# A graph attention layer: its lead-in ordered by a list scheduler with the work dealt anew, and the next to last output part finished beside the last products

## The chip, the core and the metric

One of the cores of a Trainium2 chip runs the kernel: TensorE (PE), VectorE (DVE), ScalarE (ACT) and GpSimd (POOL) compute, SyncE (SP) issues DMAs, and ACT and POOL issue some as well. Each engine runs its own instructions in the order in which they are written, and waits on semaphores where an instruction needs another engine's work. The metric is the device time of one execution in microseconds (us), as the median of several runs.

## The reference, cut to what matters

12,500 nodes with 128 features, 412,500 edges sorted by target with 64 features each, four heads of 32. Layer norm and ReLU of the nodes, a linear layer, an attention logit for each edge, a softmax over the edges of a target (which also counts the edges that are not there), a weighted sum of source rows, and the input added back:

```python
h = jnp.maximum(_layernorm(x, axis=-1), 0.0)
...
h = (node_features @ W_node.T).reshape(num_nodes, H, HD)
e = (edge_features @ W_edge.T).reshape(num_edges, H, HD)
...
att = jnp.sum(jnp.concatenate([h[src], h[tgt], e], axis=-1) * a, axis=-1)
att = jnp.where(att > 0, att, 0.2 * att)
m = jnp.maximum(jax.ops.segment_max(att, tgt, num_segments=num_nodes), 0.0)
ex = jnp.exp(att - m[tgt])
denom = segment_sum(ex, tgt) + (num_edges - deg)[:, None] * jnp.exp(-m)
return x + segment_sum((ex / denom[tgt])[:, :, None] * h[src], tgt)
```

## The kernel before, in words

**The lead-in** turns x into a table in DRAM with one row of 144 numbers a node: for each head 32 products, two ones and two logit parts. x goes through in 98 blocks of 128 rows. Blocks form groups (`sizes`, L304), up to `XB` = 9 of them, and each group has units of `XS` = 3 blocks. A group is loaded by a DMA on SP's queue (`load_rows`, L307, five buffers `xg`). A unit's steps, each by a function of its own:

- `measure` (L328, DVE): `bn_stats` of each block, and behind the group's last unit four small instructions that combine them (L337 to L341)
- `root` (L345, ACT) and `deviate` (L351, DVE): for a group, one over the standard deviation, and the shift
- `normalize` (L357): a block each on ACT (L366) or POOL (L363); units take turns with two on ACT and one on POOL, or one and two
- `turn` (L369, PE): each block transposed into PSUM tile `pt`, which is one bank with up to three blocks (three such tiles)
- `keep_turned` (L375, DVE): ReLU of the whole unit into `hT`
- `project` (L379, PE): the product with `wall`, into PSUM tile `ph` (two matmuls a block in the trace, as for every float32 matmul)
- `keep_rows` (L384): copy to `rows` on ACT (L389), and the ones by a memset on DVE (L390)
- `write` (L393): when a group is whole, its table rows by a DMA on ACT's queue, and the target logits copied to `tn` on DVE (L396)

`wall` is made from the weights by a transpose, a small matmul with `a_diag` and three copies on DVE (L425 to L435). The order of all that is a loop written by hand (from `ahead, lag = 7, 3`, L420): at unit k it projects unit k, normalises and transposes unit k + 3, measures up to unit k + 7, and applies the ReLU last. Behind the loop come `keep_near` (the target logits transposed and stored), `load_extents` and `chunk_ranges` (bounds of the edge chunks, DVE for the most part).

**The batches.** 67 batches of edges follow. For each, POOL issues 49 indirect DMAs (`gather`, L631; the last batch has fewer) that fetch table rows of the source nodes into one of four buffers `hs`. DVE and ACT make the weights, DVE multiplies the rows by them (L814), PE adds them up by target (L819), and `merge` adds what was collected to `acc` (L926). Before the first gather lies the whole table, since any row may be asked for.

**The tail.** The last batch is done in two parts (`first_part`, `second_part`). Ahead of `second_part`, `close` of the batch before merges its sums, runs `finish` (L987) for the output part that is then complete, whose stores go out on SP and ACT, and moves the open sums to the front of `acc` (`shift_sums`: a copy on DVE, L866, and a memset on POOL, L867). `second_part` then computes the weights of the last half batch (from L729), multiplies (L796), sums on PE (L803), copies the sums on ACT (L789, L790), and the last `close` merges and finishes the last part.

Of the kernel before, what the change touches and what calls it, by code (L numbers as in the profile page):

```python
# [18 lines left out]
P = 128  # L19
# [29 lines left out]
XS = 3  # L49
R = 2 * SB * H  # L50
# [75 lines left out]
def kernel(  # L126
# [110 lines left out]
    with (  # L237
# [65 lines left out]

        sizes = [XS, XS, 2 * XS] + [XB] * ((NB - 4 * XS) // XB)  # L304
        sizes += [XS, NB - sum(sizes) - XS]

        def load_rows(b0, n):  # L307

            s = Rows()
            s.b0, s.n = b0, n  # L310
            full = min(n, (N - b0 * P) // P)
            s.x = p3.tile([P, XB, D], F32, name="xg", bufs=5)
            nc.sync.dma_start(s.x[:, :full, :],
                              x[b0 * P:(b0 + full) * P, :].rearrange("(b p) d -> p b d", p=P))
            if full < n:
                nc.vector.memset(s.x[:, full, :], 0.0)
                rest = N - (b0 + full) * P
                nc.sync.dma_start(s.x[:rest, full, :], x[(b0 + full) * P:N, :])
            s.stats = p2.tile([P, XB, 2, 3], F32, name="stats", bufs=5)
            s.units = []  # L320
            for i0 in range(0, n, XS):
                u = Rows()
                u.s, u.i0, u.m = s, i0, min(XS, n - i0)
                s.units.append(u)
            return s


        def measure(u):  # L328
            s = u.s
            for i in range(u.i0, u.i0 + u.m):  # L330
                nc.vector.bn_stats(s.stats[:, i, :, :].rearrange("p a b -> p (a b)"), s.x[:, i, :])  # L331
            if u is not s.units[-1]:
                return

            n = s.n
            tot = p2.tile([P, XB, 2], F32, name="tot", bufs=5)
            nc.vector.tensor_tensor(tot[:, :n, :], s.stats[:, :n, 0, 1:], s.stats[:, :n, 1, 1:], op=OP.add)  # L337
# [5 lines left out]
            measured.append(s)  # L343

        def root(s):  # L345
            n = s.n
            s.rstd = p2.tile([P, XB], F32, name="rstd", bufs=5)
            nc.scalar.activation(s.rstd[:, :n], s.var, AF.Sqrt, bias=eps, scale=1.0 / D)
            rooted.append(s)
# [7 lines left out]
        def normalize(u):  # L357
            s = u.s
            u.hn = p2.tile([P, XS, D], F32, name="hn", bufs=4)
            for i in range(u.m):  # L360
                k = slice(u.i0 + i, u.i0 + i + 1)
                if i == XS - 1 or (i and (s.b0 + u.i0) // XS % 2):
                    nc.gpsimd.tensor_scalar(u.hn[:, i, :], s.x[:, k, :].rearrange("p b d -> p (b d)"),  # L363
                                            s.rstd[:, k], s.shift[:, k], op0=OP.mult, op1=OP.add)
                else:
                    nc.scalar.activation(u.hn[:, i, :], s.x[:, k, :].rearrange("p b d -> p (b d)"), AF.Identity,  # L366
                                         scale=s.rstd[:, k], bias=s.shift[:, k])

        def turn(u):  # L369
            pt = pps.tile([P, XS, P], F32, name="pt", bufs=3)  # L370
            for i in range(u.m):
                nc.tensor.transpose(pt[:, i, :], u.hn[:, i, :], ident)  # L372
            u.pt = pt

        def keep_turned(u):  # L375
            u.hT = p2.tile([P, XS, P], F32, name="hT", bufs=5)
            nc.vector.tensor_scalar(u.hT[:, :u.m, :], u.pt[:, :u.m, :], 0.0, None, op0=OP.max)  # L377
# [6 lines left out]
        def keep_rows(u):  # L384
# [5 lines left out]
            nc.vector.memset(rows.rearrange("p b (h k) -> p b h k", h=H)[:, :, :, HD:HD + 2], 1.0)  # L390
            return s if u is s.units[-1] else None

        def write(s):  # L393
            nc.scalar.dma_start(table[s.b0 * P:(s.b0 + s.n) * P, :].rearrange("(b p) c -> p b c", p=P),
                                s.rows[:, :s.n, :])
            nc.vector.tensor_copy(tn[:, s.b0:s.b0 + s.n, :],  # L396
# [12 lines left out]
        groups, units, measured, rooted = [], [], [], []  # L409

        def load_next():
            if len(groups) < len(sizes):
                s = load_rows(starts[len(groups)], sizes[len(groups)])
                groups.append(s)
                units.extend(s.units)

        for _ in range(5):
            load_next()
        early = [index(b) for b in range(2)]
        ahead, lag = 7, 3  # L420
        measure(units[0])
        root(measured.pop())
        deviate(rooted.pop())
        measure(units[1])
# [6 lines left out]
        nc.vector.tensor_copy(wall_h[:, :, :HD], pw.rearrange("p (h d) -> p h d", h=H))  # L431
        pa = pp1.tile([P, 2 * H], F32, name="pw")
        nc.tensor.matmul(pa, wn, a_diag[:, 0:2, :].rearrange("p j h -> p (j h)"), start=True, stop=True)
        nc.vector.tensor_copy(wall_h[:, :, AW - 1], pa[:, :H])
        nc.vector.tensor_copy(wall_h[:, :, AW], pa[:, H:])  # L435
# [59 lines left out]
        ranges = chunk_ranges()  # L495
        whole = sum(-(-n // XS) for n in sizes)
        done = 2
        full = None
        for k in range(-lag, whole + 1):
            for s in rooted:  # L500
                deviate(s)
            rooted.clear()
            u = units[k + lag] if k + lag < whole else None
            if 0 <= k < whole:
                project(units[k])
            if u:
                normalize(u)
                turn(u)
                if u is u.s.units[-1]:
                    load_next()  # L510
            if full:
                write(full)
            full = keep_rows(units[k]) if 0 <= k < whole else None
            for _ in range(2):
                if done < min(k + ahead + 1, whole):
                    measure(units[done])
                    done += 1
            if u:
                keep_turned(u)
            for s in measured:  # L520
                root(s)
            measured.clear()
            if k == whole - 4:
                early += [index(b) for b in range(2, AHEAD)]
        keep_near()
        load_extents()
        for _ in ranges:
# [254 lines left out]
    def second_part(s):  # L782
# [7 lines left out]
        nc.scalar.copy(r[:, :, 2::len(spans)], sum_part(s, *spans[1]))  # L790
# [197 lines left out]
    def finish(pool, em, b0, n, sums):  # L988
# [18 lines left out]
        def store():  # L1007
            for h in range(H):
                engine = nc.scalar if h % 2 else nc.sync
# [19 lines left out]
    def close(s):  # L1029

        first, last = merge_of(s.b)
        if s.b != last:
            return
        merge(chunk_of(first), chunks_of(first, last), *merged.pop(first))
        for b0, n, behind in parts():
# [7 lines left out]
    with tc.manual_schedule():  # L1043
# [84 lines left out]
        for store in stores:  # L1128
            store()
        stores.clear()  # L1130
# [5 lines left out]
        merged[s.b] = second_part(s)  # L1136
        close(s)
# [278 lines left out]
```

## Time and profile before

| | us |
|---|---|
| median of three runs | 4148.81 (4146.90 to 4150.61) |
| the profiled execution | 4155.16 |
| its span, first to last instruction | 4153.4 |
| POOL busy | 3093.9 (74%) |
| DVE busy | 2397.3 (58%) |
| PE busy | 1362.1 (33%) |
| ACT busy | 461.3 (11%) |
| start of the first gather | 77.37 |
| start of the last gather | 4118.11 |

The granted clock of PE was 0.658 in the mean. In the rows of the timeline, a time, a duration, the engine with the line and operation, the tile written and the tiles read, the shape and the count stand in that order; the brackets give idle time of the engine before it and what ended it. In the grouped lines, busy time and the mean of one in ns follow the first bar, idle time and its releasers the second. In a row of windows, each engine's busy time stands with its count, in the order PE, PEld (weight load), DVE, ACT, POOL; the clock, the DMA engines' mean busy share and GB/s end it. ACTq and SPq are DMA issues of the two queues.

### The profile page before, as it was taken

Reading aid. Unit: us, or ns where it says so; the run is one execution under the profiler, and the core shown is the slowest. Engines: PE = TensorE matmul, PEld = TensorE weight load, DVE = VectorE, ACT = ScalarE, POOL = GpSimd, SP = SyncE. Lnnn points to the kernel's source line nnn. Section 1 sums busy time; section 2 is a strip of 40 time slices with the busy share of each in tenths; the row PEclk is TensorE's granted clock in tenths of the full one; section 3 lists DMA queues with packets and bytes.
Section 4 is the critical chain, followed back from the end, with each engine's and each line's share of the span. In section 5 each row is a group of like instructions: output and inputs, shape, how many; then the busy total and the mean of one; then the engine's idle time right before and its main releaser. Section 6 shows DMA issues by size and latency. Waiting matters only on the chain.

```text
span 4153.4 us, 18432 instructions
## 1 busy us (share of the span) xinstructions
PE 1362.1 (33%) x3375; PEld 539.4 (13%) x3375; DVE 2397.3 (58%) x3550; ACT 461.3 (11%) x654; POOL 3093.9 (74%) x3393
## 2 busy tenths in 40 slices
PE   5332333233233233233323323323323322332331
PEld 4111111011011011111101101101101110110111
DVE  7456465456556457646555655654655654665576
ACT  4011011011101101101101110110110110111011
POOL 4777777777777777777777777777777777777775
PEclk8665666666666666566666666656656666666665
DMA  6443443443343444334444434444434434434442
GB/s 182 137 113 97 108 121 94 112 118 101 103 121 99 112 112 118 100 108 114 95 112 119 105 103 114 103 110 113 114 100 114 117 91 112 119 99 113 119 106 55
DMA packets 417256, 457.11 MB, mean 110 GB/s; under 512 B 240614, under 2 KB 324794, under 8 KB 417132
## 3 DMA queue, kind: packets, MB, share of 16 engines
q0 software_dynamic: 103136, 237.83, 24.2%
q1 hardware_dynamic: 199232, 165.73, 14.0%
q10 hardware_dynamic: 114764, 52.30, 4.7%
q14 instruction: 96, 0.79, 0.1%
q8 instruction: 28, 0.46, 0.0%
HBM read 406.51 MB, written 49.05 MB: 110 GB/s over the span
## 4 chain that ended last, share of the span: by engine, by line
POOL 73%; issue 24%; DVE 2%; PE 0%; DMA 0%; ACT 0%; POOLq 0%; ACTq 0%; SPq 0%; DVEq 0%
POOL hs L631 73%; DVE stats L331 0%; DVE hT L377 0%; POOL gate L627 0%; DMA turned<-wide 0%; DVE acc L926 0%; PE pt L372 0%; PE ph L382 0%; PE pa L803 0%; ACTq L841 0%; POOLq L631 0%; DMA hs<-table,ends 0%; DVE dif L340 0%; DVE tot L337 0%; DVE dif L341 0%
## 5 line engine op out<-in xcount | busy, mean ns | idle before, releaser
L631 POOL DMA_INDIRECT hs<-table,ends x3223 | 3059.0, 949 | 990.6 <-issue 975.6
L819 PE MATMUL pa<-hs,hot 128*128 128x504 f32 x1820 | 929.5, 676 | 2673.1 <-DVE hs L814 2673.1
L729 DVE TENSOR_TENSOR logits<-hs,pick 128x196 f32<-128x196 f32 x65 | 32.4, 499 | 1497.8 <-DVEq L648 1497.8
L819 PEld LDWEIGHTS pa<-hs,hot 128*128 128x128 f32 x1820 | 396.4, 222 | 3198.4 <-issue 3166.3
L814 DVE TENSOR_TENSOR hs<-hs,exr 128x1848 f32<-128x1848 f32 (+1 forms) x130 | 451.6, 3516 | 0.0
L744 ACT ACTIVATE both<-a 32x224 f32<-32x224 f32 (+2 forms) x268 | 103.2, 385 | 2593.7 <-DVE a L742 2583.4
L679 PE MATMUL z<-eft,wa 128*32 128x512 f32 (+1 forms) x792 | 319.6, 547 | 6.3 <-DMA eft<-in_ef 6.3
L606 DVE COPY_PREDICATED pick<-more,pick 128x1568 f32<-128x1568 int32 (+3 forms) x260 | 253.6, 975 | 8.9
L606 DVE COPY_PREDICATED pick<-more,lw 128x3136 f32<-128x3136 int32 x65 | 241.3, 3712 | 9.5 <-ACT pick L590 3.8
L590 ACT COPY pick<-lw 128x3136 f32<-128x3136 f32 x65 | 182.4, 2806 | 11.5 <-ACTq L648 9.9
L926 DVE TENSOR_TENSOR acc<-acc,up 128x70 f32 x461 | 105.2, 228 | 71.0 <-issue 52.0
L739 DVE TENSOR_TENSOR_SCAN up<-pen_sb,z 32x896 f32<-32x896 f32 (+1 forms) x67 | 133.6, 1994 | 2.3
L741 DVE TENSOR_TENSOR_SCAN m<-pen_sb,up 32x896 f32<-32x896 f32 (+1 forms) x67 | 132.6, 1979 | 2.3
L699 DVE TENSOR_TENSOR hot<-exr,key 128x1568 f32<-128x1568 f32 x65 | 116.5, 1792 | 2.3
L734 DVE TENSOR_TENSOR up<-z,zst 32x224 f32<-32x224 f32 (+2 forms) x268 | 104.3, 389 | 13.8
L679 PEld LDWEIGHTS z<-eft,wa 128*32 128x32 f32 x792 | 79.5, 110 | 242.1 <-issue 235.0
L746 DVE SCALAR_TENSOR_TENSOR both<-pen_sb,up 32x224 f32<-32x224 f32 (+2 forms) x268 | 100.2, 374 | 4.3
L856 ACT COPY r<-turned 128x245 f32<-128x245 f32 x65 | 41.5, 639 | 339.0 <-ACTq L648 295.9
L738 DVE TENSOR_TENSOR z<-up,a 32x896 f32<-32x896 f32 (+1 forms) x67 | 72.3, 1080 | 2.3
L742 DVE TENSOR_TENSOR a<-z,m 32x896 f32<-32x896 f32 (+1 forms) x67 | 71.7, 1070 | 2.3
L737 DVE TENSOR_SCALAR a<-up 32x896 f32<-32x896 f32 (+1 forms) x67 | 71.3, 1064 | 2.3
L676 PE MATMUL z<-eft,wa 128*64 128x512 f32 (+1 forms) x132 | 64.6, 571 | 21.3 <-DMA eft<-in_ef 21.3
(181 smaller groups left out, 900.3 us busy)
## 6 DMA issues: line engine op xcount, KB each, us to landing
eft<-in_ef SPq DMA_DIRECT2D x33, 1792.0 KB, 8.2
hs<-table,ends POOLq DMA_INDIRECT x3223
eft<-in_ef SPq DMA_DIRECT2D x33, 1344.0 KB
wide<-stage ACTq DMA_DIRECT2D x65, 504.0 KB, 2.9
lw<-near SPq DMA_DIRECT2D x461, 64.0 KB
pen_sb<-pens SPq DMA_DIRECT2D x66, 98.1 KB
table<-rows ACTq DMA_DIRECT2D x9, 648.0 KB, 3.6
xg<-in_x SPq DMA_DIRECT2D x52, 112.0 KB, 6.1
```

The costliest lines, as they stand in the source:

```text
L590: nc.scalar.copy(s.pick[:, :, :s.chunks, :], lw[:, None, :s.chunks, :n].to_broadcast([P, T, s.chunks, n]))
L606: nc.vector.copy_predicated(s.pick[:, :, :s.chunks, :n], bit[:, :, :, None].to_broadcast([P, T, s.chunks, n]), more)
L631: load = nc.gpsimd.indirect_dma_start(out=s.hs[:, t * CB + q, :], out_offset=None, in_=table[:, :], in_offset=bass.IndirectOffsetOnAxis(ap ...
L679: s.made = own_half(s, nc.tensor.matmul(s.z[:, part], wa3[:, j + s.b % 2 * (SB + 1), :], s.eft[:, j, part], start=False, stop=(j == NEXT - ...
L699: nc.vector.tensor_tensor(s.hot.rearrange("p t q r -> p (t q) r"), rows_ps[:, None, :].to_broadcast([P, T * CB, W]), key[:, :, None].to_br ...
L734: on_half(s, nc.vector.tensor_tensor(grouped(up, g), grouped(s.z, g), zst[g * R:(g + 1) * R, t0:t1, :], op=OP.add))
L739: on_half(s, nc.vector.tensor_tensor_scan(up[:, e0:e1], s.pen[:, e0:e1], z, 0.0, op0=OP.add, op1=OP.max))
L741: nc.vector.tensor_tensor_scan(mp[:, ::-1], s.pen[:, e1:e0:-1], up[:, e0:e1][:, ::-1], 0.0, op0=OP.add, op1=OP.max)
L744: nc.scalar.activation(both[g * R:(g + 1) * R, 0, t0:t1, :], grouped(att, g), AF.Exp)
L814: nc.vector.tensor_tensor(rows, rows, ex_ps[:, t0:t1, :CB * H, None].to_broadcast([P, t1 - t0, CB * H, HB]), op=OP.mult)
L819: scattered[s.b] = nc.tensor.matmul(wide_ps[:, g, :], s.hot[:, t, g * NEXT:g * NEXT + SB, :].rearrange("p q r -> p (q r)"), flat[:, at:at ...
L926: nc.vector.tensor_tensor(sums, sums, put[:, i0 + i, :, :], op=OP.add)
```

## The change

**1. The lead-in.** The hand-written loop is gone. `lead_in` makes a table of steps, each with its engine, a duration, a lag until others may use its result, the steps behind which it stands, and a rank; it then takes again and again the step that could start earliest by these numbers, lower rank first, and emits its instructions. The numbers set nothing but the order. The last groups get smaller (one group of three blocks goes from the front, two of six and the three and two stand at the end), and the work is dealt otherwise: of each unit's three blocks ACT normalises the first and POOL two; ACT applies the ReLU to the first block of a full unit, DVE to the rest; the memset of ones and the copy to `tn` are POOL's. Two index loads stand ahead of the x loads on SP, `a_diag` stands ahead of the first statistics on DVE, and the small matmul for `wall` has a PSUM tile of its own.

```diff
-        sizes = [XS, XS, 2 * XS] + [XB] * ((NB - 4 * XS) // XB)
-        sizes += [XS, NB - sum(sizes) - XS]
+        sizes = [XS, 2 * XS] + [XB] * 8 + [2 * XS, 2 * XS, XS, NB - 8 * XB - 8 * XS]
...
-                if i == XS - 1 or (i and (s.b0 + u.i0) // XS % 2):
+                if i < ACTS:
+                    nc.scalar.activation(u.hn[:, i, :], s.x[:, k, :].rearrange("p b d -> p (b d)"), AF.Identity,
+                                         scale=s.rstd[:, k], bias=s.shift[:, k])
+                else:
                     nc.gpsimd.tensor_scalar(u.hn[:, i, :], s.x[:, k, :].rearrange("p b d -> p (b d)"),
                                             s.rstd[:, k], s.shift[:, k], op0=OP.mult, op1=OP.add)
...
+        def keep_turned(u, own):
+            if u.hT is None:
+                u.hT = p2.tile([P, XS, P], F32, name="hT", bufs=5)
+            if own[0] < relu_acts(u):
+                for i in own:
+                    nc.scalar.activation(u.hT[:, i, :], u.pt[:, i, :], AF.Relu)
+                return
+            nc.vector.tensor_scalar(u.hT[:, own[0]:u.m, :], u.pt[:, own[0]:u.m, :], 0.0, None, op0=OP.max)
...
             nc.scalar.copy(rows, u.ph[:, :u.m, :])
-            nc.vector.memset(rows.rearrange("p b (h k) -> p b h k", h=H)[:, :, :, HD:HD + 2], 1.0)
...
+            nc.gpsimd.memset(rows.rearrange("p b (h k) -> p b h k", h=H)[:, :, :, HD:HD + 2], 1.0)
...
-            nc.vector.tensor_copy(tn[:, s.b0:s.b0 + s.n, :],
+        def keep_logits(s):
+            nc.gpsimd.tensor_copy(tn[:, s.b0:s.b0 + s.n, :],
...
+                    steps["kept", u] = Step("vector", 60 + 133 * (m - acts), 100, behind, u,
+                                            lambda u=u, a=acts: keep_turned(units[u], range(a, units[u].m)))
+                    steps["kept2", u] = Step("scalar", 300 * acts, 100, behind, u,
+                                             lambda u=u, a=acts: a and keep_turned(units[u], range(a)))
...
+            while steps:
+                at, rank, name = min((max([free[v.engine]] + [ended[k] for k in v.behind]), v.rank, name)
+                                     for name, v in steps.items() if all(k in ended for k in v.behind))
+                v = steps.pop(name)
+                free[v.engine] = at + v.busy
+                ended[name] = at + v.busy + v.lag
+                v.emit()
```

DVE's order in the middle of the lead-in before, from one reciprocal of a nine-block group to the next; numbers behind names tell buffers apart, and the brackets name the engine or DMA lane whose semaphore an instruction waits for:

```order
L377 TENSOR_SCALAR hT_652<-pt_640 128x384 [waits PE_49]
L396 COPY tn_202<-rows_594 128x36
L390 MEMSET rows_668 128x12x2 [waits DMAHW1_49,Activation_49]
L331 BN_STATS stats_424<-xg_422 128x6 x3
L377 TENSOR_SCALAR hT_674<-pt_662 128x384 [waits PE_49]
L390 MEMSET rows_668 128x12x2 [waits Activation_49]
L331 BN_STATS stats_424<-xg_422 128x6 x3
L337 TENSOR_TENSOR tot_693<-stats_424 128x18 [waits DVE_49]
L339 TENSOR_TENSOR dif_695<-stats_424 128x9
L340 SCALAR_TENSOR_TENSOR dif_695<-dif_695 128x9 [waits DVE_49]
L341 TENSOR_TENSOR dif_695<-dif_695,tot_693 128x9 [waits DVE_49]
L353 RECIPROCAL rstd_701<-rstd_701 128x9 [waits Activation_49,Pool_49]
```

The same engine at the same place after the change:

```order
L351 RECIPROCAL rstd_612<-rstd_612 128x9 [waits Pool_49]
L353 SCALAR_TENSOR_TENSOR shift_636<-tot_564,rstd_612 128x9 [waits DVE_49]
L337 TENSOR_TENSOR tot_644<-stats_400 128x18
L339 TENSOR_TENSOR dif_646<-stats_400 128x9
L340 SCALAR_TENSOR_TENSOR dif_646<-dif_646 128x9 [waits DVE_49]
L341 TENSOR_TENSOR dif_646<-dif_646,tot_644 128x9 [waits DVE_49]
L332 BN_STATS stats_468<-xg_466 128x6 [waits DMAHW0_49]
L380 TENSOR_SCALAR hT_670<-pt_654 128x256 [waits Activation_49]
L332 BN_STATS stats_468<-xg_466 128x6 x3
L380 TENSOR_SCALAR hT_681<-pt_663 128x256 [waits Activation_49]
L380 TENSOR_SCALAR hT_706<-pt_689 128x256 [waits PE_49]
L351 RECIPROCAL rstd_693<-rstd_693 128x9 [waits Activation_49,Pool_49]
```

The copy and the memsets are gone from DVE, the ReLU has 256 columns for 384 and in two units of three waits for ACT instead of PE, and the combination of the next group stands right behind `deviate`.

POOL's order before, at a nine-block group's start:

```order
L363 TENSOR_SCALAR hn_658<-xg_344,rstd_627,shift_630 128x128 [waits DVE_49,DMAHW5_49,PE_49,Activation_49]
L363 TENSOR_SCALAR hn_680<-xg_344,rstd_627,shift_630 128x128 [waits PE_49,Activation_49]
L363 TENSOR_SCALAR hn_680<-xg_344,rstd_627,shift_630 128x128
L363 TENSOR_SCALAR hn_710<-xg_344,rstd_627,shift_630 128x128 [waits PE_49,Activation_49]
L363 TENSOR_SCALAR hn_732<-xg_422,rstd_701,shift_704 128x128 [waits DVE_49,DMAHW0_49,PE_49,Activation_49]
```

And after, where `rows_642` belongs to the group ahead of the one that is normalised:

```order
L365 TENSOR_SCALAR hn_650<-xg_313,rstd_612,shift_636 128x128 [waits DMAHW4_49,DVE_49,PE_49]
L365 TENSOR_SCALAR hn_650<-xg_313,rstd_612,shift_636 128x128
L396 MEMSET rows_642 128x12x2 [waits DMAHW6_49,Activation_49]
L365 TENSOR_SCALAR hn_667<-xg_313,rstd_612,shift_636 128x128 [waits PE_49]
L396 MEMSET rows_642 128x12x2 [waits Activation_49]
L365 TENSOR_SCALAR hn_684<-xg_313,rstd_612,shift_636 128x128 [waits PE_49]
L403 COPY tn_202<-rows_642 128x36
L365 TENSOR_SCALAR hn_727<-xg_398,rstd_693,shift_713 128x128 [waits DMAHW7_49,DVE_49,PE_49]
```

Between two units' normalisations POOL now has a memset of a unit three units back, which waits for ACT's copy of it.

**2. The tail.** `close` becomes `put_together` (the merge) and `wrap_up` (finish and shift). For the next to last part `wrap_up` is called in `second_part`, behind its multiplications, and its four stores go to SP alone, behind `second_part`.

```diff
-        nc.scalar.copy(r[:, :, 2::len(spans)], sum_part(s, *spans[1]))
+        got = sum_part(s, *spans[1])
+        wrap_up(s.b - 1)
+        nc.scalar.copy(r[:, :, 2::len(spans)], got)
...
+        put_together(first, last)
+        if last != NBT - 2:
+            wrap_up(last)
...
-        for store in stores:
-            store()
-        stores.clear()
...
         merged[s.b] = second_part(s)
+        for store in stores:
+            store([nc.sync] * 2)
+        stores.clear()
         close(s)
```

DVE's order in the tail before, from the merge of the next to last part to the last merge:

```order
L926 TENSOR_TENSOR acc<-acc,up 128x70 [waits DVE_49]
L997 TENSOR_SCALAR rest<-acc 128x16 [waits DVE_49]
L1002 TENSOR_TENSOR a<-acc,exr 128x512 [waits DVE_49]
L866 COPY acc<-acc 128x420
L981 MEMSET hs 128x64 [waits PE_49]
L729 TENSOR_TENSOR logits<-hs 128x3x24 [waits DMAHW3_49,DVE_sequencer_49,late,DVE_49]
L796 TENSOR_TENSOR hs<-hs,exr 128x3x4x33 x5
L890 TENSOR_SCALAR mc<-r 128x12 [waits Activation_49]
```

And after:

```order
L964 TENSOR_TENSOR acc<-acc,up 128x70 [waits DVE_49]
L1019 MEMSET hs 128x64 [waits PE_49]
L765 TENSOR_TENSOR logits<-hs 128x3x24 [waits DMAHW3_49,DVE_sequencer_49,late,DVE_49]
L834 TENSOR_TENSOR hs<-hs,exr 128x3x4x33 x5
L1035 TENSOR_SCALAR rest<-acc 128x16
L1040 TENSOR_TENSOR a<-acc,exr 128x512 [waits DVE_49]
L904 COPY acc<-acc 128x420
L928 TENSOR_SCALAR mc<-r 128x12 [waits Activation_49]
```

The finish (L997 to L1002, now L1035 to L1040) and the copy of `acc` have moved from ahead of the half batch to behind its multiplications; what stands in between is left out here.

More of the change, by code (lines that the diff above doesn't have):

```diff
@@ L408, with relu_acts @@
         starts = [sum(sizes[:i]) for i in range(len(sizes))]
-        groups, units, measured, rooted = [], [], [], []
+        groups, units = [], []
+        def relu_acts(u):
+            return 1 if u.m == XS else 0
         def load_next():
[L412 to L418, printed above, removed]
-        early = [index(b) for b in range(2)]
@@ L420, with __init__ @@
[L420 to L424, printed above, removed]
+            s = load_rows(starts[len(groups)], sizes[len(groups)])
+            groups.append(s)
+            units.extend(s.units)
+            if len(groups) == len(sizes):
+                early.extend(index(b) for b in range(2, AHEAD))
+        class Step:
+            def __init__(self, engine, busy, lag, behind, rank, emit):
+                self.engine, self.busy, self.lag, self.behind, self.rank, self.emit = engine, busy, lag, behind, rank, emit
@@ L493, in chunk_ranges @@
             nc.vector.tensor_tensor(lastm[:, :, 0], last, lastm[:, :, 1], op=OP.subtract)
[L495 to L524, printed above, removed]
+        lead_in()
         keep_near()
         load_extents()
-        for _ in ranges:
+        for _ in chunk_ranges():
             pass
```

84 lines of the change are left out of this document (61 added, 23 removed).

## The prediction

> **What bounds the kernel now.** I read the chain of work that ended last first, then the costliest groups, then the two ends of the timeline.
>
> ```profile
> POOL 73%; issue 24%; DVE 2%; PE 0%; DMA 0%; ACT 0%; POOLq 0%; ACTq 0%; SPq 0%; DVEq 0%
> L631 POOL DMA_INDIRECT hs<-table,ends x3223 | 3059.0, 949 | 990.6 <-issue 975.6
> ```
>
> The chain is POOL's gathers (L631), 73%, and 24% in which POOL waited for nothing that the profile shows. Each gather takes 949 ns and about 0.30 us pass before the next, so 3223 of them fill about 4040 us. The first and the last of them, and the last table write ahead of the first:
>
> ```profile
> 77.37 1.15 POOL L631 DMA_INDIRECT hs<-table,ends  x1 [15.03 <-DMA near<-turned]
> 4118.11 0.95 POOL L631 DMA_INDIRECT hs<-table,ends  x1 [0.30 <-issue]
> 73.60 0.37 ACTq L394 DMA_DIRECT2D table<-rows  x1
> table<-rows ACTq DMA_DIRECT2D x9, 648.0 KB, 3.6
> ```
>
> From 77.37 to 4119.06 the stream stands for 4041.7 us, and the change leaves it alone. The time is thus the start of the first gather, plus 4041.7, plus 34.3 us from there to the end of the span at 4153.4. The row names the store of `near` as what released the first gather, but in the order of either kernel that gather waits for table writes only. The last one was issued at 73.60, and 73.60 + 3.6 (median landing) = 77.2 fits without `near`. So a lead-in that issues its last table write one microsecond earlier makes the kernel one microsecond shorter, and in the tail DVE's chain counts.
>
> **The lead-in, in groups of nine blocks.** Row blocks go through in groups, each with one `deviate` on DVE. The reciprocals of the first and the last of the nine nine-block groups:
>
> ```profile
> 15.06 0.20 DVE L353 RECIPROCAL rstd<-rstd 128x9 f32<-128x9 f32 x1
> 58.24 0.20 DVE L353 RECIPROCAL rstd<-rstd 128x9 f32<-128x9 f32 x1
> ```
>
> (58.24 − 15.06) / 8 = 5.40 us a group. What fills them on DVE, from the timeline:
>
> ```profile
> 28.17 0.26 DVE L396 COPY tn<-rows 128x36 f32<-128x36 f32 x1
> 28.63 0.27 DVE L331 BATCH_NORM_STATS2 stats<-xg 128x6 f32<-128x128 f32 x1 [0.20 <-issue]
> 28.64 0.08 DVE L390 MEMSET rows<- 128x24 f32 x1
> 28.82 0.47 DVE L331 BATCH_NORM_STATS2 stats<-xg 128x6 f32<-128x128 f32 x2
> 29.20 0.54 DVE L377 TENSOR_SCALAR hT<-pt 128x384 f32<-128x384 f32 x1
> 29.71 0.27 DVE L331 BATCH_NORM_STATS2 stats<-xg 128x6 f32<-128x128 f32 x1
> ...
> 30.39 0.18 DVE L337 TENSOR_TENSOR tot<-stats 128x18 f32<-128x18 f32 x1
> ...
> 30.98 0.55 DVE L377 TENSOR_SCALAR hT<-pt 128x384 f32<-128x384 f32 x1
> 31.50 0.22 DVE L353 RECIPROCAL rstd<-rstd 128x9 f32<-128x9 f32 x1
> 31.75 0.17 DVE L355 SCALAR_TENSOR_TENSOR shift<-tot,rstd 128x9 f32<-128x9 f32 x1
> 70.02 0.40 DVE L377 TENSOR_SCALAR hT<-pt 128x256 f32<-128x256 f32 x1 [0.65 <-PE pt L372]
> ```
>
> From start to start, three statistics take 0.57 (28.63 to 29.20), a three-block ReLU 0.51 (29.20 to 29.71), the combination 0.59 (30.39 to 30.98) and `deviate` 0.42 (31.50 to the end of the next row). With three memsets of 0.08 and the copy of 0.26, **before** needs 3 × 0.57 + 3 × 0.51 + 0.59 + 0.42 + 0.24 + 0.26 = 4.75 of the 5.40 us. The memset and the copy stand in DVE's order behind a copy on ACT, so DVE waits there with statistics queued behind them. **After**, memset and copy are on POOL, and the ReLU has two blocks: 0.54 − 0.40 = 0.14 less, 0.37. DVE: 3 × 0.57 + 3 × 0.37 + 0.59 + 0.42 = 3.83.
>
> The other engines, and the transfers:
>
> ```profile
> L363 POOL TENSOR_SCALAR hn<-xg,rstd,shift 128x128 f32<-128x128 f32 x39 | 17.1, 453 | 29.6 <-DVE shift L355 12.8 <-ACT rows L389 10.1 <-PE pt L372 6.7
> L366 ACT ACTIVATE hn<-xg,shift,rstd 128x128 f32<-128x128 f32 x37 | 16.8, 486 | 0.0
> L389 ACT COPY rows<-ph 128x432 f32<-128x432 f32 x25 | 12.7, 508 | 4.0 <-PE ph L382 3.5 <-PE pt L372 0.6
> 20.70 0.86 ACT L366 ACTIVATE hn<-xg,shift,rstd 128x128 f32<-128x128 f32 x2
> 4108.75 0.31 ACT L744 ACTIVATE both<-a 32x128 f32<-32x128 f32 x1 [5.30 <-DVE a L742]
> 6.01 0.12 POOL L214 MEMSET carry<- 128x34 f32 x1
> 38.00:44.00 6.00, 4.40 (x34) 3.81 (x34) 4.95 (x26) 3.86 (x10) 2.64 (x7) 1.00 0.83 225
> 30.00:32.00 2.00, 0.46 (x4) 0.22 (x2) 1.79 (x9) 0.90 (x3) 0.00 (x0) 1.00 1.14 332
> xg<-in_x SPq DMA_DIRECT2D x9, 576.0 KB, 6.4
> ```
>
> ACT had 37 of 76 normalisations; it gets three of nine. Two in a row take 0.86, 0.38 to 0.40 for each. A 128x128 ReLU from PSUM is not in the trace: its bounds are 0.31 (the 32x128 ACTIVATE) and 0.486 (a normalisation); I take 0.31, since it has no per-partition scale and shift to read. A copy (508 ns) overlaps its neighbour by the same 0.1, 0.41. ACT: 3 × 0.40 + 3 × 0.31 + 3 × 0.41 + 0.30 (root) = 3.66, or 4.19 with the upper bound. POOL: 6 × 0.453 = 2.72, three memsets of a strided 128x24 (not seen on POOL: 0.12 to 0.26, from its own 128x34 and DVE's copy; I take 0.12) and the copy at 0.26, 3.34 or 3.76. PE has the same work: 4.40 busy in 6 us (first column of the window 38 to 44) is 73% of 5.40, 3.95 a group. Nine blocks move 576 + 648 KB, 1.25 MB, and at the 332 GB/s of the window 30 to 32 that is 3.8 us. So **four resources stand at 3.7 to 4.0 us where one stood at 4.75**, and in-order engines that hand over to each other lose a little more. I take 4.1 us, bounds 3.95 and 5.0.
>
> What the list scheduler does not know costs part of that. In the built order DVE's ReLU of blocks 1 and 2 waits for ACT's ReLU of block 0 (in one unit of three it is the other way round), though the steps put both only behind the transpose. That is 0.31 us in a unit's way, not 0.31 us of engine time, since statistics lie ready on DVE; it is in my 4.1. The Trainium skill, "PSUM — Partial Sum Buffer", section "PSUM bank collisions raise a hardware error", says why: two engines may not use one PSUM bank and quadrant at once, two readers included, and software must order them. This rule speaks against the dealing, as one ReLU split over two engines is no faster than its parts in a row; by it the sum would be the same 4.1, and with no such rule about 4.0. The wait in the order agrees, no run here shows its time.
>
> **The ends of the lead-in.** At the start, two index loads stand ahead of the x loads on SP (0.8 us, by the 0.37 of an issue on ACT's queue), and `a_diag`, which waits for a small load, stands ahead of the first statistics. Against that, 9 blocks instead of 12 stand ahead of the first nine-block group. I put its `deviate` at 14.3 (before: 15.06), and the eighth and last one seven periods on: 14.3 + 7 × 4.1 = 43.0. Behind it ACT, the fullest engine there, has nine normalisations, eight ReLUs, eleven copies (two units are in flight) and three roots: 9 × 0.40 + 8 × 0.31 + 11 × 0.41 + 3 × 0.20 = 11.2 us. What before paid there beside work:
>
> ```profile
> 59.02 0.90 PE L382 MATMUL ph<-wall,hT 128*128 128x144 f32 x6
> 62.09 1.65 PE L382 MATMUL ph<-wall,hT 128*128 128x144 f32 x6
> 66.29 0.52 ACT L389 COPY rows<-ph 128x432 f32<-128x432 f32 x1 [1.23 <-PE ph L382]
> 68.25 0.52 ACT L389 COPY rows<-ph 128x432 f32<-128x432 f32 x1 [1.05 <-PE ph L382]
> 70.71 0.52 ACT L389 COPY rows<-ph 128x432 f32<-128x432 f32 x1 [0.76 <-PE ph L382]
> ```
>
> ACT waited for PE three times, 3.04 us, partly as the six products took 1.65 instead of 0.90 us. I allow 2.0: the small groups' statistics are done well ahead now, and the order gives ACT other units' work. Last table write 43.0 + 11.2 + 2.0 = 56.2, first gather 56.2 + 3.6 + 0.2 = **60.0**, that is 17.4 earlier.
>
> The Trainium skill, "TensorE: Matmul & The Clock Gate", section "Part 1: The HAM clock gate", says that the array falls to half clock after an idle window of about 3.4 us and rises after a busy one. The 1.65 against 0.90 fits. By the rule a lead-in that keeps PE busier keeps the full clock to its end, and the sum would lose up to 1 of the 2.0 us of waits.
>
> **The tail.** Its DVE rows, with PE and ACT where DVE waits:
>
> ```profile
> 4121.15 1.81 DVE L926 TENSOR_TENSOR acc<-acc,up 128x70 f32 x7
> 4122.99 0.18 DVE L997 TENSOR_SCALAR rest<-acc 128x16 f32<-128x16 f32 x1
> ...
> 4125.34 0.37 DVE L866 COPY acc<-acc 128x420 f32<-128x420 f32 x1
> 4125.70 0.21 DVE L729 TENSOR_TENSOR logits<-hs 128x72 f32<-128x72 f32 x1
> ...
> 4138.64 0.17 DVE L890 TENSOR_SCALAR mc<-r 128x12 f32<-128x12 f32 x1 [2.75 <-ACT r L790]
> 4138.25 0.36 ACT L790 COPY r<-pa 128x210 f32<-128x210 f32 x1 [5.56 <-PE pa L803]
> 4099.34 2.58 DMA hs<-table,ends
> ```
>
> The finish of the next to last part and the shift of the sums stand from 4122.99 to 4125.71, 2.72 us, ahead of the last half batch; later DVE idles 2.75 us for PE's products and ACT's copy. The change moves the 2.72 us behind DVE's multiplications, into that wait. The last gather ends at 4119.06 and, with the 2.58 us that an earlier half's landing took in the chain, its rows are there near 4121.6, before DVE is free at 4122.97. So the half batch starts 2.7 earlier (4123.0 for 4125.70), and the moved work just fits into the 2.75. I take 2.6, between 0 (a landing at 4125.7) and 2.7. Its four stores move behind this on SP and have 20 us until SP's last ones; POOL's memset of `acc` (1.21 us) follows the shift and has six. Without these covers each costs under 0.4 and 1.2 us.
>
> **Sum.** 17.4 + 2.6 = 20.0. The profiled execution took 4155.16 (span 4153.4): 4135.2. The median of the three runs is 6.3 lower, 4148.81; from there **4128.8, rounded 4129**.
>
> **Rivals.**
> - *The floor.* Transfers at 332 GB/s need about 41 us for 98 blocks (64 + 72 KB each), and DVE's 3.83 a group from 14.0 on puts the last `deviate` at 41; with no waits, and some of ACT's 11.2 done ahead of it, the first gather starts at 54 to 56: 4123 to 4125. For it: loads are five groups ahead. Against: every engine would be full. 0.12.
> - *Handovers eat the balance.* 4.6 to 5.0 a group (upper bound of the ReLU, transfers in each other's way: 0.83 DMA share before already) and a tail like before's: first gather 62 to 70, 4131 to 4139. 0.20.
> - *The change doesn't do what it says in the lead-in*: the order pins all to 5.3 a group by a wait that I don't see. First gather 73 to 77, 4142 to 4149. Against: the waits that DVE had are gone from its order. 0.04. *The tail alone gains nothing* (a late landing): 4131.5, inside the range.
> - *Slower.* One ring through all engines: POOL's memset of a unit waits for ACT's copy of that unit, and the next unit's normalisations queue behind it on POOL; copy waits for PE, PE for both ReLUs, these for the transpose of what POOL normalised. By rows the ring lasts 2 × 0.453 + 0.5 + 0.31 + 0.37 + 0.90 + 0.51 + 0.12 = 3.6 and some 0.7 of handovers. The memset is three units behind, so four units must last as long as the ring: 0.75 × 4.3 = 3.2 us a group, below 4.1. From 9.3 us on it would hold groups at 7.0, first gather at 14.3 + 49 + 17 = 80 and the gain of the tail used up; at 10.7, 8.0 a group, 87, 4156. 0.03.
>
> **How the numbers follow.** Forecast (first gather 56 to 62, 4125 to 4131): 0.61; the rivals as given. Eight in ten reach from the floor to most of the second rival: 4120 to 4138. About 0.2%, 8 us, is what a measurement of this kernel can tell from no change: faster by more than that (under 4140.5) 0.92, the same 0.05, slower 0.03.
>
> **What would show it.** `deviate` rows 4.0 to 4.2 apart from about 14; last table write near 56; first gather near 60, and the stream behind it still 4041 to 4042 long; in the tail no DVE wait above 0.3 us before the scan of the last merge, and 31.7 us from the last gather to the end. Wrong: DVE rows with waits for ACT's ReLU above 0.4 us each, POOL waiting in the memset, a gather stream that got longer, or a first gather beyond 62.

## The result and the profile after

| | before | after |
|---|---|---|
| median (6 runs each) | 4147.03 us (4144.45 to 4150.61) | 4130.90 us (4130.14 to 4132.51) |
| profiled execution / its span | 4155.16 / 4153.4 | 4131.72 / 4129.9 |
| first gather starts | 77.37 | 63.26 |
| last gather ends | 4119.06 | 4098.44 |
| from there to the end of the span | 34.3 | 31.5 |

The ratio is 0.9961 [0.9948, 0.9974]: 16.1 us faster, forecast 20 and inside the range. Lead-in and tail gave 14.1 + 2.9 = 17.0 us in the traces; the other 6.4 us between the two profiled executions lie inside the gather stream, and the medians, 16.1 us apart, do not show them (last section). deal_old, leadin_pad, head and best were run on a second chip, leadin_pad_b, sizes_old, ac_first and best2 on a third, where the kernel before takes 4770.37 and 4780.41 us; so their times are compared inside their own set of runs, and their lead-ins by trace.

The timeline of the changed kernel, with the rows that answer to those of before:

```profile
6.14 0.17 DVE L488 TENSOR_TENSOR a_diag<-ac,tsel 128x12 f32<-128x12 f32 x1 [1.91 <-DMA ac<-in_a_col]
15.71 0.20 DVE L351 RECIPROCAL rstd<-rstd 128x9 f32<-128x9 f32 x1
44.98 0.20 DVE L351 RECIPROCAL rstd<-rstd 128x9 f32<-128x9 f32 x1
59.67 0.91 ACTq L399 DMA_DIRECT2D table<-rows  x2
63.26 1.16 POOL L667 DMA_INDIRECT hs<-table,ends  x1 [3.13 <-DMA table<-rows]
4097.50 0.94 POOL L667 DMA_INDIRECT hs<-table,ends  x1 [0.30 <-issue]
```

The first gather is now put down to the table writes, with the wait that the order had shown. The reciprocals of the first and the eighth nine-block group lie 29.27 us apart, 4.18 a group (5.40 before). The two stretches by engine, columns as in the prediction's windows:

```profile
15.70:45.00 29.30, 26.93 (x180) 21.98 (x179) 27.00 (x132) 23.01 (x67) 20.89 (x69) 1.00 0.85 239
45.00:60.10 15.10, 12.76 (x93) 11.12 (x91) 9.69 (x45) 11.85 (x34) 9.45 (x35) 1.00 0.68 201
```

In the first, PE and DVE are both busy for 92% (26.9 and 27.0 of 29.3), ACT for 79%, POOL for 71%. In the second the granted clock is 1.00, where before it was 0.50 from 62 to 68; ACT is busy for 11.85 and idle for 3.2 of 15.1 us.

The tail: DVE's rows, then PE and ACT.

```profile
4102.40 0.28 DVE L765 TENSOR_TENSOR logits<-hs 128x72 f32<-128x72 f32 x1
4112.42 0.17 DVE L1035 TENSOR_SCALAR rest<-acc 128x16 f32<-128x16 f32 x1
...
4114.84 0.37 DVE L904 COPY acc<-acc 128x420 f32<-128x420 f32 x1
4115.21 0.17 DVE L928 TENSOR_SCALAR mc<-r 128x12 f32<-128x12 f32 x1
...
4110.70 2.44 PE L841 MATMUL pa<-hs,eft 128*32 128x35 f32 x120 [16.18 <-DVE hs L834]
4113.21 0.36 ACT L828 COPY r<-pa 128x210 f32<-128x210 f32 x1 [0.46 <-PE pa L841]
```

The half batch starts right behind the merge, the finish stands behind the multiplications, and DVE doesn't wait for ACT's copy any more. But that copy is done at 4113.57, only 1.1 us after DVE ended its multiplications and began the finish (4112.42); before, DVE waited 2.75. So some 1.6 of the 2.75 us were not filled, they are gone, and PE's rows of before show where they had been:

```profile
4115.90 0.45 PE L803 MATMUL pa<-hs,eft 128*32 128x35 f32 x13 [0.82 <-issue]
4133.94 2.41 PE L803 MATMUL pa<-hs,eft 128*32 128x35 f32 x115 [17.59 <-DVE hs L796]
4137.87 0.33 PE L803 MATMUL pa<-hs,eft 128*32 128x35 f32 x5 [1.52 <-issue]
```

Before, PE stopped for 1.52 us five products before its end (and for 0.82 us 128 products ahead of that), waiting for nothing that the profile shows; after, the 120 products go through in one piece.

### The profile page after: what moved, and what is told of

Its sections match the earlier page's. It is cut to its first block, busy times and chain, and to the rows that moved or that the text cites. A ratio compares the mean times of both kernels' runs of the same rounds, so it can differ in the third digit from the quotient of the medians.

```text
span 4129.9 us, 18410 instructions
## 1 busy us (share of the span) xinstructions
PE 1360.4 (33%) x3375; PEld 538.8 (13%) x3375; DVE 2390.1 (58%) x3503; ACT 461.0 (11%) x669; POOL 3100.1 (75%) x3457
```

## The experiments

The theory going in: the time is the start of the gathers plus the tail; the lead-in's pace is set by DVE's and PE's work; lead-in and tail add up. The rivals: the parts overlap; the pace is set by the waits through the PSUM bank that ACT and DVE share; the order alone, or the dealing alone, does it.

**One part alone.** tail_alone has the tail's diff of the section on the change on the old lead-in, leadin_alone the rest.

> The lead-in of before with the tail of the change. If the two parts are independent (theory), the first gather stays near 77.4 and the stretch from the end of the last gather to the end of the span falls from 34.3 to about 31.5, as in the changed kernel: 2.7 us under before, a ratio of 0.9993. Rival: the tail's gain needs the earlier start, or the whole gain is the lead-in's: stretch 34.3, ratio 1.000.

> The lead-in of the change with the tail of before. Theory: first gather 63.3 as in the changed kernel, stretch behind the last gather 34.3, so 14 us under before, ratio 0.9966, and 2.8 us over the changed kernel. Rival: the two parts overlap, ratio as the changed kernel, 0.9961.

Measured: tail_alone 4143.60 us, ratio 0.9993 [0.9984, 1.0002] to before at 4146.84: 3.2 us faster by the medians, not clear of no change by the interval. First gather 76.54, stretch behind the last gather 31.5. leadin_alone 4131.97, 0.9966 [0.9954, 0.9978], first gather 63.13. But its stretch is 32.6, not 34.3, and only 1.1 us separate it from the changed kernel. The rows of its tail, DVE and PE:

```profile
4123.76 0.17 DVE L926 TENSOR_SCALAR mc<-r 128x12 f32<-128x12 f32 x1 [0.94 <-ACT r L826]
...
4120.86 2.43 PE L839 MATMUL pa<-hs,eft 128*32 128x35 f32 x120 [18.86 <-DVE hs L832]
```

With the old tail and the new lead-in, DVE's wait is 0.94 us and not 2.75, since PE has no break here. tail_alone has the break, 0.97 us, and the finish covers it. So the tail's rows moved are worth 2.8 us on the old lead-in and 1.1 on the new one, and the two parts don't add up.

**Where the break comes from.** In the kernel before and in relu_dve, 128 products lie between the last two such breaks (13 and 115; 11 and 117). leadin_pad moves the place:

```diff
-        nc.tensor.transpose(pw, wn, ident)
+        for _ in range(17):
+            nc.tensor.transpose(pw, wn, ident)
```

> leadin_alone with 16 more transposes of the weights on PE, into the same PSUM tile, in the first microseconds where PE idles; nothing else. PE's rows show a break without a waited-for engine once every 128 products, 1.52 us long five products before the end of the tail in the kernel before, and none there in leadin_alone, whose stretch behind the last gather was 32.6 instead of 34.3. Theory (the break comes at a place in PE's instruction stream): 16 more products put it about 16 or 8 products before the end, and the stretch is 33.5 to 34.3 again, first gather unchanged within 0.3. Rival (it has to do with the lead-in or the run, not with the place): stretch 32.6.

> leadin_pad once more, since its first run fell on a chip where the gathers landed so late that the tail started some 130 us behind the last gather, and the stretch there says nothing. The break in PE was there nine products before the end. On a chip like the first: stretch from the end of the last gather to the end of the span 33.5 to 34.3 (leadin_alone 32.6) by the theory that the break's place costs it, 32.6 by the rival.

Measured: the ratios are 0.9965 [0.9946, 0.9983] and 0.9955 [0.9935, 0.9975]. On these two chips the stretch from the last gather says nothing, but the wait in question does. leadin_pad's DVE and PE rows, and below those of its second run:

```profile
4739.68 0.17 DVE L927 TENSOR_SCALAR mc<-r 128x12 f32<-128x12 f32 x1 [2.77 <-ACT r L827]
...
4738.88 0.35 PE L840 MATMUL pa<-hs,eft 128*32 128x35 f32 x9 [1.61 <-issue]
```

```profile
4754.82 0.17 DVE L927 TENSOR_SCALAR mc<-r 128x12 f32<-128x12 f32 x1 [2.22 <-ACT r L827]
...
4754.01 0.35 PE L840 MATMUL pa<-hs,eft 128*32 128x35 f32 x9 [1.06 <-issue]
```

Sixteen products in the first microseconds bring the break back, nine products before the end in both executions, and with it 1.8 and 1.3 us of waiting over the 0.94. It isn't the chip: without the sixteen, head on the second chip and sizes_old and ac_first on the third run these 120 products in one piece. Head's row:

```profile
4723.89 2.44 PE L846 MATMUL pa<-hs,eft 128*32 128x35 f32 x120 [17.39 <-DVE hs L839]
```

So the break belongs to a place in PE's instruction stream, and the changed lead-in had moved that place off the tail's last products. That is shown. The traces also tell what PE does in it. Among the DMA queues of before stands one that carries instructions:

```profile
q8 instruction: 28, 0.46, 0.0%
```

These are 28 packets of 16,384 bytes. In the tails there are fourteen breaks, in nine of the fourteen traces, and in each of them PE's next product starts 1.35 to 1.64 us after such a packet has landed (before: landed at 4136.35, next product at 4137.87; leadin_pad: 4737.30 and 4738.88). And the place follows the number of PE's instructions in the trace, with weight loads and semaphore instructions (waits that stand as instructions of their own): 6882 before, with the break 5 products ahead of the end; 6878 in relu_dve, with 3; 6889 in leadin_pad, with 9. Two instructions move it by one product, and 128 products with their weight loads are 256 instructions; 6882 / 256 is 26.9, near the number of packets. So PE stands where the next packet of its own instructions has come late. The changed kernel has 6857, 25 semaphore instructions fewer than before; that puts the place 120 products ahead of the end, just between the two half batches, where PE waits for DVE anyway. No run changed the packets themselves: this is read from times and counts.

**The shared PSUM bank.** relu_dve leaves the ReLU to DVE; relu_units gives ACT every third unit whole.

```diff
-            return 1 if u.m == XS else 0
+            return 0
```

```diff
-            return 1 if u.m == XS else 0
+            return units.index(u) % 3 == 1
...
-            if own[0] < relu_acts(u):
-                for i in own:
-                    nc.scalar.activation(u.hT[:, i, :], u.pt[:, i, :], AF.Relu)
+            if relu_acts(u):
+                nc.scalar.activation(u.hT[:, :u.m, :], u.pt[:, :u.m, :], AF.Relu)
```

> The changed kernel with the whole ReLU of every unit on DVE: no PSUM bank is shared by ACT and DVE, DVE gets 3 x 0.14 = 0.42 us more work in a group of nine blocks, ACT 3 x 0.28 less. Theory (DVE's and PE's work set the pace of 4.18 us): reciprocals of nine-block groups 4.4 to 4.6 apart, first gather 2 to 4 us later than 63.3, 65 to 67. Rival (what sets the pace is the ring of waits through the shared bank, 2.5 us of DVE's waits for ACT's ReLU and 4.2 us of PE's): spacing 4.0 to 4.2, first gather 61 to 63.

> The changed kernel with the same share of the ReLU on ACT, dealt by whole units: ACT takes every third unit's three blocks, DVE the other two units', so no PSUM bank has two readers and the work of each engine stays within 0.3 us a group of what it was. Theory (the waits in the shared bank cost little beside work): spacing 4.0 to 4.2, first gather 62 to 63.5. Rival (the shared bank costs most of what the lead-in lost against the prediction): spacing 3.8 to 3.9, first gather 60 to 61.

Measured: relu_dve 4132.03 us, 0.9966 [0.9953, 0.9978], first gather 63.70, pace 4.14. relu_units 4127.69 us, 0.9953 [0.9940, 0.9967], first gather 60.84, pace 3.89 (15.71 to 42.96 for seven groups). Between the first and the last of those reciprocals, the windows of relu_dve and then of relu_units:

```profile
16.98:45.98 29.00, 25.21 (x175) 21.30 (x176) 27.73 (x123) 18.77 (x47) 20.94 (x68) 1.00 0.82 231
```

```profile
15.70:42.90 27.20, 24.05 (x180) 21.65 (x180) 25.16 (x120) 22.21 (x55) 21.31 (x69) 1.00 0.91 255
```

My expectation for relu_dve fell. DVE has more ReLU work there (10.4 us in the window, 8.2 in the changed kernel's) and is busy for 96%, and still a group takes 4.14, where the changed kernel needs 4.18: DVE idles 1.3 us of 29.0 there and 2.3 of 29.3 here, so what the split ReLU saves on DVE it loses in waits. The rival's pace came (4.0 to 4.2), its first gather (61 to 63) didn't, as the first of these reciprocals was 1.3 us later.

With relu_units the rival's numbers came and mine didn't. Its first gather is 2.4 us earlier than the changed kernel's, so dealing the ReLU by whole tiles is worth that much. How much of it were waits in the shared bank isn't parted from the work, which falls too: ReLU takes 7.0 us on DVE in 13 instructions (changed kernel: 8.2 in 20) and 3.4 us on ACT in 7 (5.5 in 20), and PE's busy time is 24.1 us for 26.9; why PE's falls is not shown. DVE's idle time is nearly the same, 2.0 us for 2.3. By the medians relu_units beats the changed kernel by 3.2 us. Of the 4.0 us between the two profiled executions 1.6 lie in the tail, where the stretch behind the last gather is 29.9 and not 31.5: ACT's copy of the sums of the batch before the last waited 3.90 us for a transfer, in the changed kernel 5.57. Why is open.

**Order against dealing.** deal_old keeps list scheduler, sizes and tail and deals the work as before; sizes_old changes the sizes alone.

```diff
-                if i < ACTS:
+                if not (i == XS - 1 or (i and units.index(u) % 2)):
...
-            return 1 if u.m == XS else 0
+            return 0
...
-            nc.gpsimd.memset(rows.rearrange("p b (h k) -> p b h k", h=H)[:, :, :, HD:HD + 2], 1.0)
+            nc.vector.memset(rows.rearrange("p b (h k) -> p b h k", h=H)[:, :, :, HD:HD + 2], 1.0)
...
-            nc.gpsimd.tensor_copy(tn[:, s.b0:s.b0 + s.n, :],
+            nc.vector.tensor_copy(tn[:, s.b0:s.b0 + s.n, :],
```

```diff
-        sizes = [XS, 2 * XS] + [XB] * 8 + [2 * XS, 2 * XS, XS, NB - 8 * XB - 8 * XS]
+        sizes = [XS, XS, 2 * XS] + [XB] * ((NB - 4 * XS) // XB)
+        sizes += [XS, NB - sum(sizes) - XS]
```

> The changed kernel with the work dealt as before (two or one normalisations of a unit on ACT by turns, the whole ReLU, the memset of ones and the copy to tn on DVE); the list scheduler, its group sizes and the tail stay. Theory (DVE's work sets the pace, the dealing is the larger part): nine-block reciprocals 4.7 to 4.9 apart instead of 4.18, first gather 67 to 69. Rival (the order is what counts, DVE was idle 0.65 us of every group before): spacing 4.2 to 4.4, first gather 63 to 65. Second rival (the hand-written order was as good): spacing 5.4, 75 or more.

> The changed kernel with the group sizes of before (3, 3, 6, nine times 9, 3, 2) in the list scheduler. Theory (the sizes are a small part: as many blocks by the same engines, only the last groups' chains differ): first gather 62.5 to 65. Rival (the end of the lead-in hangs on the last groups: the last nine-block group's write of 648 KB and its nine blocks' statistics come late): 66 to 68.

Measured: deal_old 4761.42 against 4770.37 us, 0.9979 [0.9957, 1.0001], not clear of no change; sizes_old 4761.84 against 4780.41, 0.9973 [0.9951, 0.9995], first gather 64.17. deal_old's rows and window:

```profile
17.64 0.22 DVE L351 RECIPROCAL rstd<-rstd 128x9 f32<-128x9 f32 x1
...
50.36 0.18 DVE L351 RECIPROCAL rstd<-rstd 128x9 f32<-128x9 f32 x1
...
68.80 1.15 POOL L669 DMA_INDIRECT hs<-table,ends  x1 [7.88 <-issue]
```

```profile
17.60:50.40 32.80, 27.31 (x189) 22.81 (x189) 30.20 (x156) 24.19 (x60) 14.06 (x32) 1.00 0.75 215
```

Pace 4.67 and first gather 68.80, near the expected 4.7 to 4.9 and inside 67 to 69, with DVE busy for 92% and PE for 83%. But the larger share is the order's: 5.40 to 4.67 and 8.6 us of first gather by order and sizes, of which sizes about 0.9, and 4.67 to 4.18, 5.5 us, by the dealing. (The small load for `a_diag` landed at 6.64 here, at 6.14 in the changed kernel and at 5.37 in sizes_old; that is 0.5 us of the 5.5, and the sizes may be worth 0.8 more.) "The dealing is the larger part" was wrong, and DVE's busy time tells why: over the eight groups of before it is 35.6 us, 4.46 a group, and 30.2 over deal_old's seven, 4.31. The old order thus left DVE idle for 0.94 us a group and not for 0.65.

**The head.** head moves the index loads behind five x loads and `a_diag` behind the first statistics; ac_first moves the index loads alike, and the 1.5 KB load of the attention vector to the front of ACT's queue. best and best2 are these with relu_units.

```diff
-        early = [index(b) for b in range(2)]
+        early = []
...
+            if len(groups) == 5:
+                early.extend(index(b) for b in range(2))
...
+            steps["diag", 0] = Step("vector", 100, 600, [("measure", 0)], -2, spread_a)
```

```diff
+        ac = p1.tile([P, 3], F32, name="ac")
+        nc.scalar.dma_start(ac, a_col)
         wn = p1.tile([P, D], F32, name="wn")
...
-        ac = p1.tile([P, 3], F32, name="ac")
-        nc.scalar.dma_start(ac, a_col)
```

> The changed kernel with the two index loads behind the first five x loads on SP, and a_diag with its small matmul behind the first statistics. In the changed kernel the first statistics started at 6.23 (4.15 before), behind a_diag, which waited until 6.14 for its load. Theory (a late head shifts all that follows): first statistics near 4.2, the first nine-block reciprocal 1.0 to 2.0 earlier than 15.71, first gather 61.3 to 62.3 instead of 63.3. Rival (the head is caught up, since the pace is set further on): reciprocals earlier at the start and equal at the end, first gather 63.

> head and relu_units together: ReLU dealt by whole units, index loads and a_diag later. Theory (head and pace are separate terms): first gather 60.8 less 1 to 2, 59 to 60, ratio to before 0.9949 to 0.9951. Rival (the head's gain is caught up): 60.8, 0.9953.

> The changed kernel with the 1.5 KB load of the attention vector moved to the front of ACT's queue and the two index loads behind the first five x loads; a_diag stays ahead of the first statistics. In head, a_diag waited for that load until 7.76, later than in the changed kernel (6.14), since the x loads started 0.9 earlier and took its place. Theory (the small load behind other transfers makes the head late): a_diag near 4.1 without a wait, first nine-block reciprocal 13.0 to 14.2 (changed kernel 15.71), first gather 60.8 to 62.3 (63.26). Rival (caught up further on): reciprocals equal from the fourth nine-block group on, first gather 63.

> ac_first and relu_units together. Theory (head and pace are separate terms): first gather 58.3 to 59.8, 3.5 to 5 us before the changed kernel's; on a chip like the one of the first runs a time of 4125 to 4127. Rival (x loads become the bound once the head is early): first gather 60.5 to 61, as relu_units alone.

Measured: head 4753.73 against 4770.37 us, 0.9959 [0.9938, 0.9981]; best 4752.20, 0.9954 [0.9934, 0.9975]; ac_first 4758.08 against 4780.41, 0.9952 [0.9933, 0.9970]; best2 4763.59, 0.9952 [0.9929, 0.9975]. The intervals don't part these four, run two by two on two chips; the traces do. Rows of head, then of ac_first, then of best2:

```profile
7.76 0.17 DVE L497 TENSOR_TENSOR a_diag<-ac,tsel 128x12 f32<-128x12 f32 x1 [1.66 <-DMA ac<-in_a_col]
...
63.73 1.16 POOL L672 DMA_INDIRECT hs<-table,ends  x1 [3.13 <-DMA table<-rows]
```

```profile
4.15 0.17 DVE L490 TENSOR_TENSOR a_diag<-ac,tsel 128x12 f32<-128x12 f32 x1
...
62.28 1.16 POOL L669 DMA_INDIRECT hs<-table,ends  x1 [3.14 <-DMA table<-rows]
```

```profile
4.15 0.16 DVE L489 TENSOR_TENSOR a_diag<-ac,tsel 128x12 f32<-128x12 f32 x1
...
58.99 1.16 POOL L668 DMA_INDIRECT hs<-table,ends  x1 [3.39 <-DMA table<-rows]
```

head missed: with x loads that start 0.9 us earlier the small load is waited for until 7.76 and not 6.14 (7.71 in best; 4.92 to 6.64 in the eight runs with the index loads first), and the first gather came 0.5 us later. With it in front `a_diag` doesn't wait, and the first gather is 1.0 us earlier, at the weak end of what was expected; the first nine-block reciprocal, at 14.57, missed the 13.0 to 14.2. best started its gathers at 60.75 for the same reason, 0.1 earlier than relu_units and outside the expected 59 to 60. In best2 both terms add up, 4.3 us before the changed kernel's start, with a pace of 3.79. That it is faster than relu_units is open: it wasn't run on the first chip. Two runs of one kernel, on two chips, show the head's share by themselves: `a_diag` at 4.92 in leadin_pad and at 5.94 in leadin_pad_b, first gathers at 62.35 and 63.46.

## Why the prediction held, point by point

- **What bounds the kernel**: right. Gathers start when the last table write has landed, and the medians moved by what lead-in and tail gave, within 1 us.
- **DVE's work sets the pace**: right in kind. DVE is busy for 92 to 96% in the four kernels whose windows stand above; in the changed kernel PE is at 92% too, and no run parts the two there. The sum of 4.75 for the old dealing was too high: rows from start to start hold more than work, and DVE was busy for 4.46. The 3.83 for the new one fits (27.0 us over seven groups, 3.86).
- **4.1 us a group**: measured 4.18, 0.6 us late over seven groups. The rule on shared banks was priced at 0.1 us a group by hand; dealing by whole tiles brought 0.29, of which up to 0.17 is DVE's shorter ReLU work; the rest would be near the 0.1. The ReLU on ACT, put at 0.31 to 0.486, took 0.276 us, the memset on POOL 0.118, so it wasn't their price.
- **First nine-block reciprocal at 14.3**: measured 15.71. The step "`a_diag`, which waits for a small load, stands ahead of the first statistics" was named and not priced; DVE waited for the load until 6.14. In ac_first, without that wait, the reciprocal came at 14.57.
- **The end, 13.2 us from the last nine-block reciprocal to the last write**: measured about 15.1 (44.98 to the second issue of the pair at 59.67). ACT's work was 11.85 for 11.2, its idle time 3.2 for 2.0. The landing took 3.13 instead of 3.8. The clock kept full speed as hoped, but the up to 1 us of waits that this was to save didn't come: ACT idled more. In before the clock fell between 61 and 62, and PE's longest idle stretch from 55 on to there was 1.37 us, so the rows don't show the idle window that the prediction cites.
- **The first gather**: 3.3 us late, at 63.26, outside the 56 to 62 of the forecast's case and inside the 62 to 70 of the second rival, though the pace was not that rival's 4.6 to 5.0. It was a sign of being wrong by the prediction's own list, and two others came: DVE waited for ACT's ReLU for up to 0.6 us at a time, and POOL in the memset. The mechanism held, the sizes of head and end were off, and the 4130.90 us lie in the forecast's 4125 to 4131 by 0.1 us.
- **The tail, 2.6 us**: measured 2.9, right by luck, from a sum with one wrong part. The move itself is worth 1.1 us beside the new lead-in; the other 1.7 are the PE break that went elsewhere. I took a row's 2.75 us of waiting as a gap that stays, though PE's own "issue" stood in it; 25 semaphore instructions fewer ahead of it took that away.
- **The slower rival**: its sign came and its cost didn't. POOL's memsets waited for ACT's copies, 7.0 us in all from 14 to 60, but POOL was busy for only 71% of the first stretch, and the pace stayed at 4.18.

## What to carry to other kernels

When a gap is to be filled, look at what is in it: here a part of DVE's wait was PE standing at a place in its instruction stream, and it was gone once instructions ahead of it were fewer. Take an engine's work from its busy time in a window and not from rows laid start to start. Price the first loads of a kernel like work: DVE waited 0.7 to 2.4 us for a load of 1.5 KB behind bigger ones. Deal work over engines by whole PSUM tiles, and let the scheduler know each wait that the tiles bring; a split that left two readers in one bank needed more instructions and paid for its saving with waits.

## What else the runs showed of the hardware

**Small DVE instructions with two SBUF inputs got longer beside POOL.** The combination's rows from 14 to 60 us, of before and of after:

```profile
L341 DVE TENSOR_TENSOR dif<-dif,tot 128x9 f32<-128x9 f32 x9 | 1.5, 170 | 0.3
```

```profile
L341 DVE TENSOR_TENSOR dif<-dif,tot 128x9 f32<-128x9 f32 x8 | 1.9, 233 | 0.3
```

The same instruction took 0.40 us at 18.09 while POOL normalised. Of the 48 rows of the combination after, 34 overlap a normalisation on POOL, and 16 of these took more than 200 ns; of the 14 others none took more than 172. The Trainium skill, "SBUF — State Buffer", section "Who interferes with whom", says that a DVE instruction with two SBUF inputs contends with a GpSimd instruction that reads SBUF. The rows agree for DVE; on POOL's side nothing shows, its normalisations stayed at 448 ns (453 before).

**The gather stream has two lengths.** First and last gather of leadin_alone:

```profile
63.13 1.17 POOL L667 DMA_INDIRECT hs<-table,ends  x1 [3.13 <-DMA table<-rows]
...
4105.04 0.94 POOL L667 DMA_INDIRECT hs<-table,ends  x1 [0.30 <-issue]
```

Over 3222 steps that is 1.2545 us each, as in the profiled execution of before (1.2541); in the changed kernel it is 1.2521. That makes 6 to 8 us, half of what the change brought, and leadin_alone's profiled execution (4140.35 us) lies as far above its median of 4131.97. What sets it is open.

**A chip can be otherwise.** On the second and third the granted clock was 0.63 in the mean and gathers were issued nearly as fast (951 to 954 ns each), but POOL waited ahead of a batch at the memset that guards its buffer, in deal_old some 40 times for over 1 us and 500 us in all. The gain of the changed lead-in was still there (ratios of 0.9952 to 0.9965, and 0.9973 with the old sizes).
